# One copy of q, k and v from PSUM to SBUF in layer 1's main loop

## The chip, the cores and the metric

The kernel runs on one core of a Trainium2 chip, as one launch. The metric is the device time of one execution in microseconds. Three executions of the kernel before took 9888.43, 9790.23 and 9846.99 us; their median is 9846.99. A further execution was taken with the hardware profiler, and all durations below come from that one.

## The reference, cut to what matters

The input `x` is four images of 64 x 64 positions with 128 channels, float32. Four layers follow each other:

- Layer 0 is a deformable attention: q, k and v from a 3 x 3 depthwise convolution, offsets from q, gathers of k and v at nine sampled places for each of four heads, a softmax over the nine, and a projection.
- Layer 1 is a linear attention. Of `qkv = x @ w_qkv` it takes a softmax of q over each head's 32 channels, a softmax of k over all 4096 positions, the context `k^T v`, and `context @ q` projected, normalized and added to its input:

```python
q = softmax(q, axis=-1) / sqrt(32)      # 4 heads of 32
k = softmax(k, axis=1)                  # over the positions
context = einsum('bnhd,bnhe->bhde', k, v / n)
out = einsum('bhde,bnhd->bnhe', context, q)
```

- Layer 2 is a gated attention and a mixture of 64 experts with eight positions for each.
- Layer 3 is a causal linear attention and a spectral filter bank (the long convolution with 16 filters).

Every layer works on a normalized input and adds to its residual. The change lies in layer 1.

## The kernel before, in words

**Two streams of work.** `hybrid` runs layer 0 image by image: 8 chunks of 512 positions, four tiles a chunk, four heads a tile, so 128 attention steps an image and 512 in all. I call such a step a group. A group (`attend`, L606 to L662) issues nine gathers on POOL (L619, into one of three `gt` buffers), multiplies and reduces on DVE (L628, L633 to L638), takes one exponential on ACT (`ex`, L642), and multiplies and reduces on DVE again (L646, L651, L654). `front` prepares the next image beside it; it makes two chunks of q (`image`, L462) ahead of the table of k and v (`table`, L422), and the other six behind it.

**The background.** While image b is in layer 0, `Post.run(b - 1)` takes the image before through layers 1 to 3. It is a chain of Python generators; each `yield` hands out a number, the cost of the piece just written, and `hybrid` draws from it until the sum reaches 1176 x (groups so far) / 128, thus 9.19 units a group. Layer 1's loop yields 5.0 in each of its sixteen passes; a chunk of layer 3's attention (L1207 to L1287, eight of them, each with two L1222) yields 5.0 + 4.0 + 4.0. Image 3 has no next image: after its layer 0 the last `Post.run` stands alone (I call it the tail), with `wide` set, which gives it more buffers.

**What sets the order.** The program is written in this interleaved order, but a planner decides at build time in which order each engine's queue holds its instructions: of those whose inputs it takes to be ready it issues first what stands earlier in the text, and an engine that would be idle takes what stands later. On the chip each queue is run in that order. A background that is written early and becomes ready late is therefore issued behind attention groups that stand behind it in the text. At two places the order is tied by hand through `Turns` (L60 to L78): each `ex` is issued on ACT behind the last ACT instruction recorded for "behind" (L640), and the filter bank's copies (L1440) behind that for "samples" (L1439). "Behind" is recorded only while `paced` is set, and that happens at L828, where `stu_tokens` begins, until the image's background ends.

**Layer 1's main loop** (L879 to L915) handles two tiles of 128 positions a pass. PE makes q, k and v of a tile in one matmul into PSUM (`pq`, L883, a bank for each tile; `ps_qkv` has one buffer beside layer 0 and two in the tail). DVE subtracts the maximum from k (L888), ACT takes its exponential (L889). DVE sets a column of ones in `v1` (L891), ACT copies v into it (L892), and PE adds `ek^T v1` to the context (`pc`, L899), so that the column of ones gives the sum of the softmax. For q, DVE reduces the maximum of each head (L895) and subtracts it (L897), ACT takes the exponential (L903), DVE sums, inverts and multiplies (L905 to L907), PE transposes (L910) and ACT copies the result to `qT` (L914). L888, L892, L895 and L897 read `pq` in PSUM.

Of the kernel before, what the change touches and what calls it, by code (L numbers as in the profile page):

```python
# [16 lines left out]
P = 128  # L17
# [3 lines left out]
C = 128  # L21
# [698 lines left out]
class Post:  # L720
# [115 lines left out]
    def layer1(self, xa, xaT, st, xb):  # L836
        nc, k, w = self.nc, self.k, self.w
        with ExitStack() as outer:
            keep = self.pool(outer, "l1keep", 1)
            sm = self.pool(outer, "l1sm", 1)  # L840
            qT = keep.tile([P, N], F32, name="qT")
            w2 = keep.tile([P, C], F32, name="w2")
            with ExitStack() as ctx:
                big = self.pool(ctx, "l1big", 1)
                wk = self.pool(ctx, "l1wk", 2)
                ps = self.psum(ctx, "l1tr", 2, 3)
                ps_qkv = self.psum(ctx, "l1qkv", 1, 2)
                ps_ctx = self.psum(ctx, "l1ctx", 1, 1)
                xT = big.tile([P, N], F32, name="xT1")
                for c in range(8):  # L850
                    part = slice(c * 512, (c + 1) * 512)
                    nc.sync.dma_start(xT[:, part], xaT[:, part])
                yield 5.0
                rs = groupnorm(nc, k, sm, ps, st)
                for h in range(4):
                    part = xT[:, h * 1024 : (h + 1) * 1024]
                    nc.scalar.activation(part, part, AF.Identity, bias=rs[:, 1:2], scale=rs[:, 0:1])
                yield 5.0


                mx = sm.tile([P, 9], F32, tag="mx", name="mx")
                for c in range(8):
                    pk = ps.tile([P, 512], F32, tag="p", name="pk")
                    nc.tensor.matmul(
                        pk, lhsT=w.qkv1[:, C : 2 * C], rhs=xT[:, c * 512 : (c + 1) * 512],
                        start=True, stop=True,
                    )
                    nc.vector.tensor_reduce(mx[:, c : c + 1], pk, AX.X, ALU.max)
                    yield 1.5
                nc.vector.tensor_reduce(mx[:, 8:9], mx[:, 0:8], AX.X, ALU.max)  # L870
                dg = sm.tile([P, P], F32, tag="dg", name="dg")
                nc.vector.tensor_scalar_mul(dg, k.ident, mx[:, 8:9])
                pm = ps.tile([P, 512], F32, tag="p", name="pm")
                nc.tensor.matmul(pm[:, :P], lhsT=k.ones, rhs=dg, start=True, stop=True)
                mrow = sm.tile([P, 1, P], F32, tag="mrow", name="mrow")
                nc.scalar.copy(mrow[:, 0, :], pm[:, :P])


                pc = ps_ctx.tile([P, 512], F32, tag="p", name="pc")  # L879
                for i in range(0, NT, 2):  # L880
                    pq = ps_qkv.tile([P, 2, 512], F32, tag="p", name="pq")
                    for u in range(2):
                        nc.tensor.matmul(  # L883
                            pq[:, u, : 3 * C], lhsT=xT[:, (i + u) * P : (i + u + 1) * P],
                            rhs=w.qkv1, start=True, stop=True,
                        )
                    ek = wk.tile([P, 2, C], F32, tag="ek", name="ek")
                    nc.vector.tensor_sub(ek, pq[:, :, C : 2 * C], mrow.to_broadcast([P, 2, P]))  # L888
                    nc.scalar.activation(ek, ek, AF.Exp)  # L889
                    v1 = wk.tile([P, 2, C + 1], F32, tag="v1", name="v1")  # L890
                    nc.vector.memset(v1[:, :, C : C + 1], 1.0)  # L891
                    nc.scalar.copy(v1[:, :, :C], pq[:, :, 2 * C : 3 * C])  # L892
                    qh = pq[:, :, :C].rearrange("p u (h c) -> p u h c", h=4)
                    qm = wk.tile([P, 2, 4], F32, tag="qm", name="qm")
                    nc.vector.tensor_reduce(qm, qh, AX.X, ALU.max)  # L895
                    eq = wk.tile([P, 2, 4, 32], F32, tag="eq", name="eq")
                    nc.vector.tensor_sub(eq, qh, qm.unsqueeze(3).to_broadcast([P, 2, 4, 32]))  # L897
                    for u in range(2):
                        nc.tensor.matmul(  # L899
                            pc[:, : C + 1], lhsT=ek[:, u, :], rhs=v1[:, u, :],  # L900
                            start=(i + u == 0), stop=(i + u == NT - 1),
                        )
                    nc.scalar.activation(eq, eq, AF.Exp)  # L903
                    qs = wk.tile([P, 2, 4], F32, tag="qs", name="qs")
                    nc.vector.tensor_reduce(qs, eq, AX.X, ALU.add)  # L905
                    nc.vector.reciprocal(qs, qs)
                    nc.vector.tensor_mul(eq, eq, qs.unsqueeze(3).to_broadcast([P, 2, 4, 32]))  # L907
                    pt = ps.tile([P, 512], F32, tag="p", name="pt")
                    for u in range(2):
                        nc.tensor.transpose(  # L910
                            pt[:, u * P : (u + 1) * P], eq[:, u].rearrange("p h c -> p (h c)"),
                            k.ident,
                        )
                    nc.scalar.copy(qT[:, i * P : (i + 2) * P], pt[:, : 2 * P])  # L914
                    yield 5.0  # L915


                rk = sm.tile([P, 1], F32, tag="rk", name="rk")
                nc.vector.reciprocal(rk, pc[:, C : C + 1])
                cx = sm.tile([P, P], F32, tag="cx", name="cx")  # L920
                nc.vector.scalar_tensor_tensor(cx, pc[:, :C], rk, k.heads, ALU.mult, ALU.mult)
                pt = ps.tile([P, 512], F32, tag="p", name="pt")
                nc.tensor.transpose(pt[:, :P], cx, k.ident)
                cxT = sm.tile([P, P], F32, tag="cxT", name="cxT")
                nc.scalar.copy(cxT, pt[:, :P])
                pw = ps.tile([P, 512], F32, tag="p", name="pw")
                nc.tensor.matmul(pw[:, :C], lhsT=cxT, rhs=w.out1, start=True, stop=True)
                nc.scalar.copy(w2, pw[:, :C])
                yield 6.0


            with ExitStack() as ctx:
                yp = self.pool(ctx, "l1y", 2 if self.wide else 1)
                wk = self.pool(ctx, "l1wk2", 2)
                ps = self.psum(ctx, "l1o", 3, 4)
                n2 = self.norm[0]
                for half in range(2):
                    y = yp.tile([P, 16, C], F32, tag="y", name="y")
                    ny = Norm(nc, k, sm, 16, "ny")
                    for c in range(4):  # L940
                        i = 16 * half + 4 * c
                        po = ps.tile([P, 512], F32, tag="p", name="po")
                        for u in range(4):
                            nc.tensor.matmul(
                                po[:, u * P : (u + 1) * P],
                                lhsT=qT[:, (i + u) * P : (i + u + 1) * P], rhs=w2,
                                start=True, stop=True,
                            )
                        nc.vector.tensor_add(
                            y[:, 4 * c : 4 * c + 4, :], po.rearrange("p (u c) -> p u c", u=4),  # L950
                            w.bout.unsqueeze(1).to_broadcast([P, 4, C]),
                        )
                        for u in range(4):
                            ny.add(4 * c + u, y[:, 4 * c + u, :])
                        yield 3.0
                    ny.finish()
                    for c in range(4):
                        x = self.load(wk, xa, 4 * half + c)
                        yc = y[:, 4 * c : 4 * c + 4, :]
                        for u in range(4):  # L960
                            ny.apply(4 * c + u, yc[:, u, :], yc[:, u, :])
                        nc.vector.tensor_mul(yc, yc, w.lns.unsqueeze(1).to_broadcast([P, 4, C]))
                        nc.vector.tensor_add(x, x, yc)
                        for u in range(4):
                            n2.add(16 * half + 4 * c + u, x[:, u, :])
                        nc.sync.dma_start(chunk(xb, 4 * half + c), tiles(x))
                        yield 3.0
                n2.finish()
# [896 lines left out]
```

## Time and profile before

| what | value |
|---|---|
| median of three executions | 9846.99 us |
| profiled execution, its own time | 9880.9 us |
| its span, first to last instruction | 9879.2 us |
| busy PE / weight loads / DVE / ACT / POOL | 5958.9 / 4119.0 / 4642.4 / 2260.0 / 4397.7 us |
| mean granted TensorE clock | 0.761 of full speed |
| first `ex` of images 0, 1, 2, 3 | 272, 1944, 4194, 6461 us |
| layer 1's loop, first to last L883: images 0, 1, 2, 3 of the background | 2010 to 2137, 4292 to 4426, 6560 to 6698, 8674 to 8711 us |

How to read what follows. A line of the groups names source line, engine, operation, output and inputs, their sizes, and the number of instructions, then busy time and mean nanoseconds of one, then how long the engine was idle just before them and what ended that. A line of the timeline gives start and duration in microseconds and, in brackets, the idle time before and its releaser. A line of a source line's own view gives the least, median and greatest duration in nanoseconds. In the table of stages each engine's busy microseconds stand with the number of its instructions, then the granted clock, the share of the DMA engines and their rate.

### The profile page before, as it was taken

The page shows a single profiled execution, that of the slowest core. Times are in us where ns is not written, and L with a number is a line of the kernel's source. Part 1 is how long each engine was busy: PE and PEld are TensorE (multiplying, and loading weights), DVE is VectorE, ACT ScalarE, POOL GpSimd, SP SyncE. Part 2 cuts the span into 40 slices and gives each one's busy share as a digit, 9 for nine tenths or more (in the row PEclk, how much of TensorE's full clock was granted, in tenths as well). Part 3 has the DMA queues.
Part 4 walks back from the last instruction along what each step waited for, and adds up shares of the span by engine and source line. Part 5 has one row for each costly group of instructions (what it writes and reads, how often), then busy time and mean ns, then how long its engine had stood idle before and what let it go on. Part 6 is the DMA issues. An engine that isn't in the chain of part 4 may idle for free.

```text
span 9879.2 us, 87205 instructions
## 1 busy us (share of the span) xinstructions
PE 5958.9 (60%) x30347; PEld 4119.0 (42%) x30347; DVE 4642.4 (47%) x7777; ACT 2260.0 (23%) x4190; POOL 4397.7 (45%) x4736
## 2 busy tenths in 40 slices
PE   7355200056685767756676667744455767757899
PEld 5133100024354545524344445522243555534676
DVE  1545555465454444466454444466454444443222
ACT  3100000023222222223122222213222222232222
POOL 0666666654535455554434445555535445400000
PEclk9677555567787888867787888865677888867999
DMA  6534433334645444454645444444635444444323
GB/s 214 147 111 115 115 103 103 101 105 145 202 123 156 114 115 117 113 140 144 185 140 144 109 114 116 118 135 142 192 117 150 114 111 116 111 136 130 107 68 81
DMA packets 1131344, 1263.41 MB, mean 128 GB/s; under 512 B 392990, under 2 KB 915481, under 8 KB 1126681
## 3 DMA queue, kind: packets, MB, share of 16 engines
q1 hardware_dynamic: 907309, 652.59, 24.1%
q0 software_dynamic: 221184, 604.27, 21.2%
q8 instruction: 240, 3.93, 0.2%
q14 instruction: 199, 1.63, 0.1%
q10 hardware_dynamic: 2412, 0.98, 0.0%
HBM read 1061.76 MB, written 195.61 MB: 127 GB/s over the span
## 4 chain that ended last, share of the span: by engine, by line
PE 34%; another core or an unknown queue 22%; issue 11%; DVE 9%; ACT 7%; POOL 5%; DMA 3%; SPq 1%; DVEq 0%; ACTq 0%; POOLq 0%
PE pa L1450 13%; PE pq L1426 5%; POOL gt L619 5%; ACT y L1440 3%; PE pm L435 2%; DVE o L654 2%; PE ph L1135 1%; DVE pr L628 1%; DMA xin<-x 1%; PE pm L470 1%; DVE s L633 1%; PE pq L883 1%; DVE pv L651 1%; PE pm L512 1%
## 5 line engine op out<-in xcount | busy, mean ns | idle before, releaser
L619 POOL DMA_INDIRECT gt<-tbl,idx x4608 | 4388.7, 952 | 4162.4 <-DVE pv L651 2386.1
L1450 PE MATMUL pa<-y,m 128*128 128x256 f32 x8192 | 2125.9, 412 | 165.8 <-issue 151.4
L1450 PEld LDWEIGHTS pa<-y,m 128*128 128x128 f32 x8192 | 1631.6, 205 | 646.8 <-issue 404.9
L1440 ACT COPY y<-pq 128x1024 f32<-128x1024 f32 x896 | 869.7, 1015 | 2310.4 <-remote 1328.2
L1426 PE MATMUL pq<-th,xh 32*128 32x256 f32 x8192 | 713.1, 452 | 696.8 <-ACT y L1440 473.3
L646 DVE TENSOR_TENSOR qa<-cw,ex 128x36 f32<-128x36 f32 x512 | 104.0, 203 | 2160.0 <-ACT ex L642 1967.3
L654 DVE TENSOR_REDUCE o<-pv 128x32 f32<-128x1152 f32 x512 | 1076.2, 2102 | 12.8 <-remote 9.7
L435 PE MATMUL pm<-wd,xT 128*128 128x256 f32 x2376 | 661.1, 424 | 279.1 <-ACT kv L446 178.0
L1426 PEld LDWEIGHTS pq<-th,xh 32*128 32x128 f32 x8192 | 430.8, 209 | 909.5 <-ACT y L1440 516.6
L628 DVE TENSOR_TENSOR pr<-gt,qa 128x1152 f32<-128x1152 f32 x512 | 690.4, 1348 | 219.2 <-DMA gt<-tbl,idx 186.3
L651 DVE TENSOR_TENSOR pv<-gt,qa 128x1152 f32<-128x1152 f32 x512 | 691.8, 1351 | 35.7 <-DVE qa L646 14.7
L633 DVE TENSOR_REDUCE s<-pr 128x36 f32<-128x1152 f32 x512 | 687.8, 1343 | 0.6
L435 PEld LDWEIGHTS pm<-wd,xT 128*128 128x128 f32 x2376 | 484.0, 212 | 459.8 <-ACT kv L446 202.6
L642 ACT ACTIVATE ex<-sc,mx 128x9 f32<-128x9 f32 x512 | 156.8, 306 | 1125.3 <-DVE mx L638 508.8
L1437 DVE COPY y<-pq 128x1024 f32<-128x1024 f32 x128 | 156.8, 1225 | 466.0 <-ACT y L1440 466.0
L470 PE MATMUL pm<-xT,wd 128*128 128x512 f32 x576 | 294.2, 661 | 133.4 <-issue 76.5
L588 PE MATMUL qa<-sident,qt 128*128 128x128 f32 x256 | 54.4, 340 | 456.8 <-issue 324.5
L1135 PE MATMUL ph<-w,pooled 128*1 128x512 f32 x512 | 238.3, 781 | 46.9 <-DMA w<-in_L_ffn_weight_dram 35.1
L588 PEld LDWEIGHTS qa<-sident,qt 128*128 128x128 f32 x256 | 45.2, 235 | 476.7 <-issue 336.5
L1149 DVE TENSOR_TENSOR g<-pt,b1T 128x16 f32<-128x16 f32 x64 | 11.2, 175 | 487.7 <-PE pt L1144 406.4
L670 PE MATMUL pt<-ident,o 128*128 128x128 f32 x128 | 31.6, 336 | 335.5 <-DVE o L661 118.0
L147 ACT ACTIVATE ln<-xin,ln,ln 128x128 f32<-128x128 f32 x512 | 211.3, 483 | 98.9 <-DMA xin<-x 67.7
(377 smaller groups left out, 6514.4 us busy)
## 6 DMA issues: line engine op xcount, KB each, us to landing
w<-in_L_ffn_weight_dram SPq DMA_DIRECT2D x512, 256.0 KB
th<-th SPq DMA_DIRECT2D x512, 256.0 KB
gt<-tbl,idx POOLq DMA_INDIRECT x4608
xin<-x SPq DMA_DIRECT2D x224, 256.0 KB
x<-xin SPq DMA_DIRECT2D x160, 256.0 KB
tbl<-kv SPq DMA_DIRECT2D x264, 128.0 KB
th<-wx SPq DMA_DIRECT2D x32, 1024.0 KB
q<-qd SPq DMA_DIRECT2D x288, 64.0 KB
```

Source lines behind the costliest of these rows:

```text
L147: self.nc.scalar.activation(dst, src, AF.Identity, bias=self.shift[:, i : i + 1], scale=self.rstd[:, i : i + 1])
L435: nc.tensor.matmul(pm[:, t, :], lhsT=self.xf[:, at : at + P], rhs=self.wd[:, tap, C:], start=(t == 0 and tap == 0), stop=False,)
L470: nc.tensor.matmul(pv, lhsT=self.wd[:, tap, :C], rhs=self.xT[:, 8 * c + dy : 8 * c + dy + 8, dx : dx + HW], start=(tap == 0), stop=False,)
L619: nc.gpsimd.indirect_dma_start(out=gt[:, i, :], out_offset=None, in_=self.tbl[b % 2][:, :], in_offset=bass.IndirectOffsetOnAxis(ap=blk.idx ...
L628: nc.vector.tensor_mul(pr, corners[:, :, 0:32], qa[:, q0 + 32 * g : q0 + 32 * g + 32].unsqueeze(1).to_broadcast([P, 4 * K2, 32]),)
L633: nc.vector.tensor_reduce(s4, pr, AX.X, ALU.add)
L651: nc.vector.tensor_mul(pv, corners[:, :, 32:64], aw.unsqueeze(2).to_broadcast([P, 4 * K2, 32]),)
L654: nc.vector.tensor_reduce(o[:, t, 32 * g : 32 * g + 32], pv.rearrange("p i s -> p s i"), AX.X, ALU.add)
L1135: nc.tensor.matmul(ph[32 * j : 32 * j + 1, :], lhsT=pooled[:, 16 * j + q : 16 * j + q + 1], rhs=w1s[j], start=True, stop=True,)
L1426: nc.tensor.matmul(pq[:, r // 2, r % 2, :, pair, :], lhsT=xh[rows, 2 * (q % 4) + pair, :], rhs=t[rows, 2 * (q % 2) + pair, :].rearrange("p ...
L1440: nc.scalar.copy(to, src)
L1450: nc.tensor.matmul(pa[:, h * 2 * P : (h + 1) * 2 * P].rearrange("p (g x) -> p g x", g=8), lhsT=s.m[u][:, KC * kc + i, :], rhs=yv[:, i], st ...
```

## The change

Two buffers `qkv0` and `qkv1` of 2 x 385 elements in each partition are made before the loop, and their last column is set to one there. In each pass ACT copies q, k and v of both tiles (2 x 384 elements) from PSUM into one of them in turn. The steps that read `pq` now read that buffer, v with its column of ones is a part of it, and the tile `v1` with its memset and its copy is gone. All source lines behind the loop stand four lines further down.

```diff
+                qkv = [big.tile([P, 2, 3 * C + 1], F32, name=f"qkv{i}") for i in range(2)]
+                for t in qkv:
+                    nc.vector.memset(t[:, :, 3 * C :], 1.0)
                 pc = ps_ctx.tile([P, 512], F32, tag="p", name="pc")
                 for i in range(0, NT, 2):
                     pq = ps_qkv.tile([P, 2, 512], F32, tag="p", name="pq")
...
+
+                    sb = qkv[i // 2 % 2]
+                    nc.scalar.copy(sb[:, :, : 3 * C], pq[:, :, : 3 * C])
                     ek = wk.tile([P, 2, C], F32, tag="ek", name="ek")
-                    nc.vector.tensor_sub(ek, pq[:, :, C : 2 * C], mrow.to_broadcast([P, 2, P]))
+                    nc.vector.tensor_sub(ek, sb[:, :, C : 2 * C], mrow.to_broadcast([P, 2, P]))
                     nc.scalar.activation(ek, ek, AF.Exp)
-                    v1 = wk.tile([P, 2, C + 1], F32, tag="v1", name="v1")
-                    nc.vector.memset(v1[:, :, C : C + 1], 1.0)
-                    nc.scalar.copy(v1[:, :, :C], pq[:, :, 2 * C : 3 * C])
-                    qh = pq[:, :, :C].rearrange("p u (h c) -> p u h c", h=4)
+                    v1 = sb[:, :, 2 * C :]
+                    qh = sb[:, :, :C].rearrange("p u (h c) -> p u h c", h=4)
                     qm = wk.tile([P, 2, 4], F32, tag="qm", name="qm")
```

## The prediction

> **What bounds the kernel now.** I read the page first, then the busy time of each engine by stage, then the times of one instruction that every attention step issues (`ex`, L642, 512 of them), then the loop that the change edits. I call one `ex` a group and count them from 0; image b of layer 0 owns groups 128b to 128b+127. From the page:
>
> ```profile
> PE 34%; another core or an unknown queue 22%; issue 11%; DVE 9%; ACT 7%; POOL 5%; DMA 3%; SPq 1%; DVEq 0%; ACTq 0%; POOLq 0%
> L619 POOL DMA_INDIRECT gt<-tbl,idx x4608 | 4388.7, 952 | 4162.4 <-DVE pv L651 2386.1
> L1440 ACT COPY y<-pq 128x1024 f32<-128x1024 f32 x896 | 869.7, 1015 | 2310.4 <-remote 1328.2
> ```
>
> No engine owns the chain. POOL, which issues layer 0's gathers, is idle as long as it works, and most of that idle time ends when the attention's DVE step L651 hands a buffer back. The stages, with each engine's busy time and the granted clock:
>
> ```profile
> core 0: us, PE busy (x) PEld busy (x) DVE busy (x) ACT busy (x) POOL busy (x), PEclk, DMA share, GB/s
> 272.00:1943.00 1671.00, 431.67 (x1295) 273.52 (x1295) 912.77 (x1291) 107.19 (x371) 1095.27 (x1151) 0.61 0.39 112
> 1944.00:4194.00 2250.00, 1498.20 (x7528) 1025.24 (x7528) 1103.93 (x1860) 585.81 (x1075) 1108.39 (x1166) 0.78 0.48 132
> 4292.00:4460.00 168.00, 94.80 (x319) 55.21 (x318) 108.88 (x255) 42.09 (x112) 86.73 (x91) 0.73 0.31 90
> 5103.00:5220.00 117.00, 105.97 (x570) 75.72 (x568) 76.74 (x222) 47.91 (x94) 8.72 (x9) 0.97 0.22 66
> 8674.00:8718.00 44.00, 37.21 (x166) 22.76 (x164) 33.97 (x116) 23.70 (x67) 0.00 (x0) 1.00 0.76 228
> ```
>
> Row 1 is image 0, with no layers 1 to 3 behind it: 1671 / 127 = 13.2 us a group, POOL busy 66%. Row 2 is image 1 with the background: 17.6 us a group, no engine above 67%. So the background is paid as delay in queues, not as work on a full engine. Row 3 is the edited loop of the second background image, row 5 the same loop in the tail, where layer 0 is over. Row 4 is the important one: POOL does 8.7 us of work in 117. The chain there, in order of time:
>
> ```profile
> 5102.69 0.30 ACT L642 ACTIVATE ex<-sc,mx 128x9 f32<-128x9 f32 x1
> ...
> 5220.32 0.30 ACT L642 ACTIVATE ex<-sc,mx 128x9 f32<-128x9 f32 x1
> ...
> 5223.44 0.94 POOL L619 DMA_INDIRECT gt<-tbl,idx  x1 [106.83 <-DVE pv L651]
> ```
>
> This is the hold. From `stu_tokens` on (L828 sets `paced`) each `ex` stands on ACT's queue behind the background's last ACT instruction, so at group 310 the attention stands still until all of layer 3 is through: 117.6 us for one group, with 16 L1222, two to a chunk, so eight chunks of layer 3. The other images have the same hold: 2870.29 to 2971.35 (101.1 us, six chunks) and 7293.82 to 7421.51 (127.7 us, seven). What lies in a hold is background that came late.
>
> **The edited loop, priced.**
>
> ```profile
> L883 PE MATMUL pq<-wqkv,xT x256: 486/840/1006, 2011.0 to 8711.7; 128*128 128x384 f32 x128
> L892 ACT COPY v<-pq x64: 352/356/378, 2024.5 to 8713.0; 128x256 f32<-128x256 f32 x64
> L897 DVE TENSOR_TENSOR eq<-pq,qm x64: 364/417/426, 2025.4 to 8714.6; 128x256 f32<-128x256 f32 x64
> L907 DVE TENSOR_TENSOR eq<-eq,qs x64: 394/419/478, 2032.3 to 8716.3; 128x256 f32<-128x256 f32 x64
> ...
> 8709.72 0.41 DVE L897 TENSOR_TENSOR eq<-pq,qm 128x256 f32<-128x256 f32 x1
> 8710.05 0.19 DVE L906 RECIPROCAL qs<-qs 128x8 f32<-128x8 f32 x1
> 8710.27 0.43 DVE L907 TENSOR_TENSOR eq<-eq,qs 128x256 f32<-128x256 f32 x1
> 8710.61 0.42 DVE L905 TENSOR_REDUCE qs<-eq 128x8 f32<-128x256 f32 x1
> ```
>
> *Copy.* 64 copies of 256 elements (356 ns) become 64 of 768. The 1024-element copy at L1440 takes 1015 ns, so 356 + 512 x (1015 - 356) / 768 = 795 ns: 64 x 0.44 = 28 us more on ACT. ACT is busy 26% of image 1's stretch and 54% in the tail's loop, so I charge nothing for the work itself; without that cover it costs 28 us. But every DVE step of the loop now queues behind this copy, and the copy behind whatever ACT has ahead of it, a waiting `ex` included; that delay is in the loop terms below.
>
> *DVE's sources.* Three of its steps a pass read SBUF in place of PSUM. L897 (PSUM) lets the next start after 0.33 us, L907 (SBUF) after 0.34; durations 417 and 419. I charge 0. [...]
>
> *Memsets.* 64 of 60 ns become 8; they lie in DVE's idle time, 0 (at most 4 us).
>
> *PSUM comes free early.* `pq` has one buffer while layer 0 runs. Before, the next L883 waits for L897 (in row 3's stretch PE waited 10.6 us for it in five waits); after, for the copy alone, and two `qkv` buffers let a second pass start. This matters through the planner. With the two programs laid side by side, engine by engine, the changed one issues the loop differently: for image 1 still two passes a group, for images 2 and 3 sixteen passes within groups 264 to 268 and 392 to 396 (nine and seven in the densest), where they filled 265 to 273 and 393 to 402. What follows moves forward, and at the hold two of eight chunks of layer 3 already stand ahead of it for image 2, four of eight for image 3 (one before); image 1's hold keeps its six. From group 311 and 439 on, the ACT order of the background is the old one.
>
> **The sum.**
>
> 1. *Holds.* Five chunks leave them (two, three). In the hold a chunk takes (117.6 - 13.2) / 8 = 13.1 us, so 65 us go. Beside attention they cost something: the first 52 groups of the second background image take 17.2 us each, 4.0 over the quiet 13.2, and carry 9.19 units of the program's own pacing (1176 / 128); a chunk has 13 units (5 + 4 + 4), so 5.7 us each, 28 back. Net -37. The other end: the 101.1 us hold has two chunks less than the 117.6 one and is only 16.5 shorter, 8.3 a chunk, net -13. I take -37, since it is the mean of the very stretch that shrinks.
> 2. *Dense loops.* What sixteen passes cost above quiet groups: image 1, 147.8 us for ten groups, 16 over; image 2, 167.3 for nine, 48 over; image 3, 171.4 for ten, 39 over. A dense loop has no row beside attention; the nearest is the tail, where a pair of passes takes 4.84 us (L888 at 8701.27 and 8706.11), 16 x 2.42 = 39. Image 2: 39 - 48 = -9; image 3: 0. The low end is image 1's 16 (-32 and -23, together -55), the high end below (+28 and +37, together +65).
> 3. *Image 1's loop.* Same spacing: 0. Its 16 us could vanish (-16), or the copy's 0.8 us could show in each pass (+13).
> 4. *Tail loop.* DVE idles about 0.8 us in each 4.84 us pair, waiting for ACT and PE; steady order one pass at a time, -2 (0 to -5).
> 5. *Table loads.* The exp, square root and gelu steps change places once more each way on ACT for image 2: 2 x 1.28 = +3.
>
> Together -37 - 9 + 0 - 2 + 3 = -45. Against the profiled execution's own 9880.9 us that is 9836. It lay 34 above the median of the three runs (9847.0), so the forecast is **9802 us**. The runs spread over 98 us, so a change under about 1% can hardly be told from none.
>
> **Rivals.**
>
> *A: dense matmuls make the loop cheap.* For: L883 takes 840 ns at the median and 486 in the tail, and the granted clock is 0.73 in row 3, 1.00 in row 5. If the dense loop runs as in the tail and hides beside attention as image 1's does, the low end of term 2 holds: 9802 - 46 = 9756. Against: DVE needs 16 x 2.29 us (five steps of 0.42 and one of 0.19) beside four attention steps of 6.9 (L651, L628, L633 and L654: 1.35 + 1.35 + 1.34 + 2.10, and 0.8 of small ones). Chance 0.20. [...]
>
> *B (slower): the dense loop holds the attention.* DVE runs in order, and in group 265 some thirty loop steps now stand between the attention's L628 and L638. At the cold pace PE needs 2.90 + 1.23 + 0.63 = 4.76 us a pass (the rows at 4311.71, 4309.77 and 4310.79), 76 us for sixteen, all of it added if POOL's three buffers are full meanwhile: +65 for the two images, +13 for image 1, holds at their low end -13, so +65: 9912. It decides from a pass of about 3.8 us on (61 us for sixteen, then term 2 is +35 and outweighs the holds). Chance 0.20.
>
> *C: nothing moves.* The work that leaves a hold reappears in full before it, as 17.6 us a group whatever the spacing: 9847. Chance 0.12.
>
> [...] Chance 0.03.
>
> Forecast: 0.45. The range takes A and most of B, with the spread of the runs: 9705 to 9930. Faster by over 1% (under 9749) needs A and a lucky median: 0.20. Slower by over 1% (over 9945) needs B with more than its price, or a stall that the rows don't show: 0.12. Within 1%: 0.68.
>
> **What the profile after would show.** the new copy near 795 ns x64; the steps of L895 and L897 still 417 ns; the hold of image 2 near 90 us, image 3's near 90, image 1's still 101; sixteen passes of images 2 and 3 in some 60 us and the clock above 0.73 there; the tail's pair at 4.5 to 4.8 us. I am wrong if a group in 264 to 268 lasts over 45 us (B), or if the holds shrink and the groups ahead of them grow by as much (C).

## The result: 0.5% faster, and the profile after

| | before | after |
|---|---|---|
| median, same chip | 9869.34 us | 9813.69 us |
| lowest and highest of 19 executions each | 9790.23, 9919.02 | 9775.16, 9850.76 |
| span of the profiled execution | 9879.2 us | 9819.3 us |

The ratio is **0.9947, with a 95% interval of 0.9926 to 0.9968**: 56 us less. That is under the 1% that I took for the bound of what can be told, but with this many executions the interval stays clear of 1. Forecast were 45 us less.

The changed kernel's page, its span, its chain and its two costliest groups (columns as explained above; lines behind the loop are four higher):

```profile
span 9819.3 us, 87113 instructions
...
PE 33%; another core or an unknown queue 26%; issue 12%; DVE 9%; ACT 7%; POOL 6%; DMA 4%; SPq 1%; DVEq 0%; ACTq 0%; POOLq 0%
...
L619 POOL DMA_INDIRECT gt<-tbl,idx x4608 | 4389.1, 953 | 4114.9 <-DVE pv L651 2351.1
...
L1444 ACT COPY y<-pq 128x1024 f32<-128x1024 f32 x896 | 869.5, 1015 | 2279.5 <-remote 1318.7
```

The shape is that of before: POOL idles nearly as long as it works, and most of its idle time still ends at L651. POOL's idle time is 47.5 us shorter (4162.4 before), most of what the span lost. The table of stages of the changed kernel: image 0 alone, image 1 with the background, the groups 264 to 267 that hold the loop of the second background image, the holds of images 2 and 3, and the loop in the tail:

```profile
core 0: us, PE busy (x) PEld busy (x) DVE busy (x) ACT busy (x) POOL busy (x), PEclk, DMA share, GB/s
272.00:1941.00 1669.00, 425.86 (x1295) 271.36 (x1295) 913.53 (x1292) 107.28 (x371) 1097.13 (x1152) 0.61 0.39 112
1942.00:4193.00 2251.00, 1487.16 (x7531) 1021.22 (x7532) 1101.07 (x1847) 592.10 (x1077) 1106.38 (x1162) 0.79 0.47 131
4299.00:4398.00 99.00, 67.77 (x255) 40.42 (x254) 67.89 (x163) 40.53 (x91) 43.15 (x45) 0.83 0.22 68
5111.00:5212.00 101.00, 90.48 (x455) 62.00 (x454) 64.05 (x188) 40.29 (x81) 8.97 (x9) 0.96 0.21 66
7316.00:7386.00 70.00, 47.38 (x275) 37.59 (x274) 41.86 (x117) 26.51 (x52) 8.70 (x9) 0.91 0.19 59
8624.00:8663.00 39.00, 35.79 (x166) 22.28 (x164) 33.75 (x103) 30.18 (x67) 0.00 (x0) 0.98 0.88 264
```

The same four groups (264 to 267) in the kernel before, where eight copies of v (L892) start in them instead of sixteen of `qkv`:

```profile
4292.00:4364.00 72.00, 39.67 (x112) 21.69 (x111) 48.13 (x104) 20.72 (x53) 41.91 (x45) 0.69 0.29 86
```

PE's work in these groups went from 39.7 us to 67.8, the granted clock from 0.69 to 0.83, and the stretch from 72 us to 99. Rows four and five are the holds. In order of time, in the changed kernel, the `ex` of images 2 and 3 ahead of the hold and behind it, and POOL's first gather afterwards with its idle time:

```profile
5110.69 0.30 ACT L642 ACTIVATE ex<-sc,mx 128x9 f32<-128x9 f32 x1 [2.89 <-DVE mx L638]
...
5211.78 0.30 ACT L642 ACTIVATE ex<-sc,mx 128x9 f32<-128x9 f32 x1
...
5214.89 0.94 POOL L619 DMA_INDIRECT gt<-tbl,idx  x1 [90.35 <-DVE pv L651]
...
7315.65 0.30 ACT L642 ACTIVATE ex<-sc,mx 128x9 f32<-128x9 f32 x1 [3.24 <-DVE mx L638]
...
7385.91 0.30 ACT L642 ACTIVATE ex<-sc,mx 128x9 f32<-128x9 f32 x1
...
7388.20 0.94 POOL L619 DMA_INDIRECT gt<-tbl,idx  x1 [59.12 <-DVE pv L651]
```

Image 2's hold is 101.1 us long (117.6 before), image 3's 70.3 (127.7 before, where POOL idled 115.51 us). The whole account, from the starts of `ex` in both profiles; the last column has the same differences on another chip, between the kernel whose order up to the tail is that of before (e_tail below) and the changed kernel (after_again):

| stretch (groups) | before | after | difference | on another chip |
|---|---|---|---|---|
| image 1: loop (128 to 140) | 215.0 | 221.7 | +6.7 | -13.5 |
| image 1: ahead of the hold (140 to 181) | 711.6 | 707.4 | -4.2 | -8.0 |
| image 1's hold (181) | 101.1 | 101.5 | +0.4 | -0.2 |
| image 2: loop (256 to 273) | 265.4 | 278.3 | +12.9 | +17.7 |
| image 2: ahead of the hold (273 to 309) | 643.1 | 639.9 | -3.2 | -17.5 |
| image 2's hold (309) | 117.6 | 101.1 | -16.5 | -16.5 |
| image 3: loop (384 to 402) | 267.9 | 278.4 | +10.6 | +23.4 |
| image 3: ahead of the hold (402 to 437) | 564.7 | 591.6 | +26.9 | -0.5 |
| image 3's hold (437) | 127.7 | 70.3 | -57.4 | -45.9 |
| the rest of layer 0, where the order is the same | 5332.7 | 5309.2 | -23.5 | +1.9 |
| tail | 1260.1 | 1246.9 | -13.2 | -5.0 |
| sum | | | -60.5 | -64.1 |

In both pairs the holds shrink by as much as the total or more (-73.5 and -62.6) and the dense loops take some of it (+23.5 and +41.1). The 23.5 us of the unchanged stretches in the first pair lie within what executions of one kernel differ by (129 us between the lowest and the highest before), so of that pair's 60 us some 24 are placed by the order (all rows but these and the tail's); in the second pair nearly all are. Ahead of image 3's hold the first pair lost 26.9 us and the second nothing. In that stretch the first pair has groups of over 28 us, three before (408, 416, 432) and six after (404, 416, 420, 422, 425, 432); the second has none.

### The profile page after: what moved, and what is told of

Same layout as the page of the kernel before. It is cut to its first block, busy times and chain, and to the rows that moved or that the text cites. A ratio compares the mean times of both kernels' runs of the same rounds, so it can differ in the third digit from the quotient of the medians.

```text
span 9819.3 us, 87113 instructions
## 1 busy us (share of the span) xinstructions
PE 5912.5 (60%) x30347; PEld 4102.3 (42%) x30347; DVE 4635.2 (47%) x7721; ACT 2288.4 (23%) x4192; POOL 4398.1 (45%) x4736
## 4 chain that ended last, share of the span: by engine, by line
PE 33%; another core or an unknown queue 26%; issue 12%; DVE 9%; ACT 7%; POOL 6%; DMA 4%; SPq 1%; DVEq 0%; ACTq 0%; POOLq 0%
PE pa L1454 13%; POOL gt L619 6%; PE pq L1430 5%; ACT y L1444 4%; PE pm L435 2%; DVE o L654 2%; PE ph L1139 1%; DVE pr L628 1%; DMA gt<-tbl,idx 1%; DVE s L633 1%; DVE pv L651 1%; PE pm L470 1%; DMA xin<-x 1%; PE pa L1250 1%
## 5 line engine op out<-in xcount | busy, mean ns | idle before, releaser
L1444 ACT COPY y<-pq 128x1024 f32<-128x1024 f32 x896 | 869.5, 1015 | 2279.5 <-remote 1318.7
L654 DVE TENSOR_REDUCE o<-pv 128x32 f32<-128x1152 f32 x512 | 1076.2, 2102 | 8.5 <-DVE qa L646 2.7
L435 PE MATMUL pm<-wd,xT 128*128 128x256 f32 x2376 | 653.8, 422 | 278.4 <-ACT kv L446 193.9
L628 DVE TENSOR_TENSOR pr<-gt,qa 128x1152 f32<-128x1152 f32 x512 | 690.1, 1348 | 253.2 <-DMA gt<-tbl,idx 232.5
L651 DVE TENSOR_TENSOR pv<-gt,qa 128x1152 f32<-128x1152 f32 x512 | 691.8, 1351 | 24.0 <-DVE qa L646 8.6
L147 ACT ACTIVATE ln<-xin,ln,ln 128x128 f32<-128x128 f32 x512 | 211.2, 482 | 97.8 <-DMA xin<-x 77.0
```

The costliest lines, as they stand in the source:

```text
L147: self.nc.scalar.activation(dst, src, AF.Identity, bias=self.shift[:, i : i + 1], scale=self.rstd[:, i : i + 1])
L435: nc.tensor.matmul(pm[:, t, :], lhsT=self.xf[:, at : at + P], rhs=self.wd[:, tap, C:], start=(t == 0 and tap == 0), stop=False,)
L628: nc.vector.tensor_mul(pr, corners[:, :, 0:32], qa[:, q0 + 32 * g : q0 + 32 * g + 32].unsqueeze(1).to_broadcast([P, 4 * K2, 32]),)
L651: nc.vector.tensor_mul(pv, corners[:, :, 32:64], aw.unsqueeze(2).to_broadcast([P, 4 * K2, 32]),)
L654: nc.vector.tensor_reduce(o[:, t, 32 * g : 32 * g + 32], pv.rearrange("p i s -> p s i"), AX.X, ALU.add)
L1444: nc.scalar.copy(to, src)
```

## The experiments

The main comparison and the last group of four experiments were run on chips where the kernel before takes about 9870 us; the others ran on two chips where the kernel before takes 7799.05 and 7795.84 us, so each ratio is taken against the kernel before on the same chip, and only differences are carried across.

My theory, H: the gain is the shorter holds, and they are shorter because `pq` comes free early, so that the planner issues the loop sooner. The rivals, as letters in the expectations: P, the packed passes themselves pay; M, the memsets; T, the tail; D, DVE's steps gain by reading SBUF in place of PSUM; N, the holds cost nothing; E, the copy pays because ACT does it; and L, which was formed on the way, that what counts is how late the background is at the point where the attention is first tied to it.

| run | edit in a word | ratio (95%) | us | hold of image 2, 3 |
|---|---|---|---|---|
| e_psumsrc | k and q read from PSUM again | 0.9979 (0.9969 to 0.9989) | -18 | 114.6, 113.5 |
| e_onebuf | one `qkv` buffer | 0.9948 (0.9931 to 0.9964) | -40 | 95.8, 70.6 |
| e_narrow | not in the tail | 0.9923 (0.9906 to 0.9939) | -56 | 95.5, 70.7 |
| e_ones | only the column of ones is set once | 1.0013 (1.0002 to 1.0023) | +9 | 114.6, 123.4 |
| after_again | the changed kernel | 0.9910 (0.9893 to 0.9926) | -69 | 97.5, 70.7 |
| e_tail | only in the tail | 0.9995 (0.9985 to 1.0005) | -2 | 114.0, 116.6 |
| b_nohold | before, `paced` set later | 1.0009 (0.9999 to 1.0018) | +6 | 93.9, 102.0 |
| a_nohold | after, `paced` set later | 0.9941 (0.9921 to 0.9961) | -46 | 86.3, 59.4 |
| b_late28w | before, the tie two groups later | 0.9931 (0.9909 to 0.9953) | -71 | 103.8, 94.6 |
| a_late28w | after, the tie two groups later | 0.9843 (0.9822 to 0.9864) | -164 | 92.1, 25.3 |
| a_late46w | after, the tie three groups later | 0.9859 (0.9837 to 0.9881) | -142 | 104.7, 32.9 |
| e_dvecopy | the copy on DVE | 0.9966 (0.9947 to 0.9984) | -35 | 101.1, 74.1 |

Microseconds are differences of medians within a group; the groups are the first four, the next four, the last four.

### Which part of the change pays

**e_psumsrc.** The copy stays, but DVE reads k and q from `pq` as before, so that `pq` is held as long as ever.

```diff
-                    nc.vector.tensor_sub(ek, sb[:, :, C : 2 * C], mrow.to_broadcast([P, 2, P]))
+                    nc.vector.tensor_sub(ek, pq[:, :, C : 2 * C], mrow.to_broadcast([P, 2, P]))
...
-                    qh = sb[:, :, :C].rearrange("p u (h c) -> p u h c", h=4)
+                    qh = pq[:, :, :C].rearrange("p u (h c) -> p u h c", h=4)
```

> The copy of q, k and v and the column of ones stay as in the change, but DVE's steps for q and k read PSUM again, so that PSUM is freed as late as before. The planned order falls back to that of before: two passes a group in images 2 and 3, eight chunks of layer 3 in the hold of image 2 and seven in that of image 3. Theory H (the gain is layer 3 leaving the holds because PSUM comes free early): holds near 118 and 128 us again, nothing gained, 0 to +20 us against the kernel before (28 us more ACT work, beside other work). Rival O (one wide copy in place of a copy and a memset is what pays): half or more of the 56 us stays. The DVE steps take 417 ns from either memory, so rival D (SBUF sources) would show as a longer median of these steps here than in the change.

The planned order falls back to two passes a group, the holds to six, eight and seven chunks, and most of the gain goes; 18 us stay (interval -24 to -9), which H did not give it. By one profile of each, e_psumsrc is 8.5 us shorter than e_tail in image 1's loop (groups 128 to 140) and 6.2 us between it and the hold; the cause was not settled. In its trace, POOL's first gather behind the holds of images 2 and 3:

```profile
4091.27 0.94 POOL L619 DMA_INDIRECT gt<-tbl,idx  x1 [103.76 <-DVE pv L651]
...
5696.44 0.94 POOL L619 DMA_INDIRECT gt<-tbl,idx  x1 [96.11 <-DVE pv L651]
```

The changed kernel on a chip of the same speed (after_again) has these lines instead:

```profile
4066.75 0.94 POOL L619 DMA_INDIRECT gt<-tbl,idx  x1 [87.21 <-DVE pv L651]
...
5656.68 0.94 POOL L619 DMA_INDIRECT gt<-tbl,idx  x1 [59.74 <-DVE pv L651]
```

So the bank's early release changes the order, and with the order go the holds. Whether the order alone would do it, with the bank held as long as before, was not tested.

**e_onebuf.**

```diff
-                qkv = [big.tile([P, 2, 3 * C + 1], F32, name=f"qkv{i}") for i in range(2)]
+                qkv = [big.tile([P, 2, 3 * C + 1], F32, name=f"qkv{i}") for i in range(1)]
...
-                    sb = qkv[i // 2 % 2]
+                    sb = qkv[0]
```

> The change with one qkv buffer instead of two. The planned loop is less dense (3 to 5 passes a group in images 2 and 3 instead of up to 9 and 7), but the holds have the same six and four chunks as in the change. Theory H: holds near 101 and 70 us as in the change, and the loop stretches of images 2 and 3 cost less than the change's 278 and 278 us (5 to 15 us each), so -55 to -75 us against before. Rival P (the second buffer and the dense loop are what pays): half or more of the gain goes, -30 us or less.

Two to five passes a group now, and the holds are as short as with two buffers. But the loops did not get cheaper by being spread: groups 256 to 273 took 232.7 us and 384 to 402 247.9 (235.3 and 244.8 in after_again), and PE's idle time ahead of L886 that ended with the copy went from 42.3 us to 107.9. The gain, -40 us beside the -56 of e_narrow on the same chip, is less than H gave and more than P: the early release carries most of it, and the second buffer perhaps the rest (the two intervals overlap a little).

**e_narrow and e_tail.** The old and the new form of the loop stand under a condition:

```diff
+                    if not self.wide:
+                        sb = qkv[i // 2 % 2]
+                        nc.scalar.copy(sb[:, :, : 3 * C], pq[:, :, : 3 * C])
...
+                    else:
+                        ek = wk.tile([P, 2, C], F32, tag="ek", name="ek")
+                        nc.vector.tensor_sub(ek, pq[:, :, C : 2 * C], mrow.to_broadcast([P, 2, P]))
```

> The change in the three loops beside layer 0 only; the tail keeps the old loop. The planned order up to the tail is that of the change. Theory H: the holds as in the change (101, 70 us), the start of the tail as early as in the change (45 us or so before that of the kernel before), and only the tail's 13 us missing: -35 to -50 us. Rival T (the tail loop, which lies alone on the path, brings most): less than half of the gain, -25 us or less.

> The change in the tail only; the three loops beside layer 0 keep the old loop, and the planned order up to the tail is that of before: holds with six, eight and seven chunks. Theory H: holds near 96, 115 and 114 us as before, only the tail's share, 0 to -13 us. Rival T (the tail loop, alone on the path, brings most): -28 us or more.

(e_tail has the condition the other way round.) Without the tail's part the gain is -56 us, with the tail's part alone -2: the tail pays next to nothing, and T falls. (The -56 lies a little beyond the 35 to 50 that I expected.)

**e_ones.** The kernel before with two `v` buffers whose last column is set once:

```diff
+                vs = [big.tile([P, 2, C + 1], F32, name=f"vs{i}") for i in range(2)]
+                for t in vs:
+                    nc.vector.memset(t[:, :, C:], 1.0)
...
-                    v1 = wk.tile([P, 2, C + 1], F32, tag="v1", name="v1")
-                    nc.vector.memset(v1[:, :, C : C + 1], 1.0)
+                    v1 = vs[i // 2 % 2]
```

> The kernel before with only the column of ones moved: two v buffers with the column set once, v copied as before, q and k from PSUM. The planned order is that of before but for one chunk: the hold of image 3 has eight chunks of layer 3 instead of seven, that of image 2 eight as before. Theory H: holds near 118 and 135 to 140 us, 0 to +15 us against before. Rival M (the 56 memsets that go out of the loop pay): -5 us or more, with the holds as before.

The memsets are worth nothing, and M falls; the 9 us on the other side go with one more chunk of layer 3 in image 3's hold, 123.4 us against the 116.6 of e_tail, whose order up to the tail is that of before (135 to 140 were expected).

**e_dvecopy.**

```diff
-                    nc.scalar.copy(sb[:, :, : 3 * C], pq[:, :, : 3 * C])
+                    nc.vector.tensor_copy(sb[:, :, : 3 * C], pq[:, :, : 3 * C])
```

> The change with its copy on DVE instead of ACT. The planned loop is the densest of all (14 passes in one group), the holds have six, six and four chunks as in the change. 64 copies of 768 elements on DVE, at the 0.33 us that 256 take from one start to the next about 0.8 us each, 53 us of DVE work in all. Theory L: holds near 95, 97 and 70 us as in the change, so most of the gain stays; the loops cost 10 to 20 us more each and the tail 10: -15 to -45 us against before. Rival E (ACT's nearness or idleness is what pays): nothing left, 0 us or slower.

The DVE copy takes 959 ns, 64 of them 61 us on the engine that the attention needs, and the kernel is still 35 us faster than before, with the holds that the table shows. Group 264 takes 53.2 us and group 392 53.6 here. E falls: which engine frees the bank matters little for the holds.

**after_again**, the changed kernel beside these on another chip:

> The changed kernel itself, beside the others of this call. Its planned order up to the tail is that of the kernel that keeps the old loop in the tail, which took 0.9923 of the kernel before. Theory H: holds of 95 to 101 us with six chunks (images 1 and 2) and 70 us with four (image 3), -50 to -65 us against before. Rival T (the tail brings more): -75 us or more.

Here 69 us go (interval -83 to -58; expected were 50 to 65), where the main comparison has 56, from a total that is a fifth shorter. A gain in per cent would have scaled with the total; this one did not. That fits with a hold having hardly any gathers in it (POOL worked 9 of 101 us).

### Is it the holds, or what stands behind them?

**b_nohold and a_nohold** set `paced` later, so that `ex` is tied to the background only from the filter bank on:

```diff
-            self.paced = True
             yield from self.stu_tokens(stu, xa, self.u[b % 2], xb)
+        self.paced = True
         yield from self.stu_filters(stu, self.u[b % 2], xb, out[b])
```

> The kernel before with the tie of each ex to the background set one stage later, where the filter bank begins and no longer where the token stage begins: in the planned order layer 3's chunks lie one or two to a group in 310 to 316 (182 to 188, 437 to 444), and the eight token steps come at once at group 316 instead. Theory H: no group above 60 us at 181, 309 and 437; a chunk beside attention costs some 5 us where it took 9.5 to 14 in the hold, and a new, shorter hold of about 45 us for the token steps comes at 316: -20 to -100 us against before. Rival N (a hold costs nothing, since the attention makes up for it afterwards): within 15 us of before.

> The changed kernel with the same later tie. Theory H: with no hold for layer 3 to leave, the change is worth less than half of what it is with the hold: -5 to -25 us against the kernel before with the later tie (whose run is in the same call). Rival P (the gain comes from the loop itself, wherever layer 3 ends): -45 us or more against it.

This is the experiment that went against H as I had worded it. If the tie at L828 made the hold, the kernel before should gain by losing it, and the change should have little left to bring. Neither came: the change still brings 52 us, which is the number that rival P gave for this run. But P's reason fails, for the loops cost more here as well (+16.9 us in groups 264 to 273 and +24.3 in 392 to 402). The holds at 181, 309 and 437 do vanish in the kernel before (14.9 to 17.1 us remain), and new ones stand where the tie now begins, at groups 187, 315 and 443, of 85.5, 93.9 and 102.0 us. The time is within 6 us of before, which is what N gave; but N's reason is wrong, for the idle time is there, in another place. POOL's gathers behind the new holds of images 2 and 3 in b_nohold:

```profile
4176.24 0.94 POOL L619 DMA_INDIRECT gt<-tbl,idx  x1 [82.05 <-DVE pv L651]
...
5784.04 0.94 POOL L619 DMA_INDIRECT gt<-tbl,idx  x1 [90.50 <-DVE pv L651]
```

In a_nohold, with the change:

```profile
4155.49 0.94 POOL L619 DMA_INDIRECT gt<-tbl,idx  x1 [72.49 <-DVE pv L651]
...
5741.98 0.94 POOL L619 DMA_INDIRECT gt<-tbl,idx  x1 [48.30 <-DVE pv L651]
```

The change again takes the most from image 3's (102.0 to 59.4 us), and 50 us from the three together. Hence theory L: a hold is the background's lateness, paid at the first place where the attention is tied to it, wherever that is; the change makes the background less late.

**b_late28w, a_late28w, a_late46w** test L without touching the loop. An idle piece of 28 (or 46) units ahead of layer 3, with as much added to the total, lets two (or three) more groups stand ahead of the tie in the text, while a background that is late catches up:

```diff
             yield from self.layer2_ffn(xa, xb)
+            yield 28.0
             yield from self.layer3_attn(xb, xa)
...
-WORK = 1176.0
+WORK = 1204.0
```

> The kernel before, its loop untouched, with a pause of 28 units (three groups of attention) written between layer 2 and layer 3, and the pacing stretched by the same 28 units. In the planned order the hold of image 1 keeps six chunks, that of image 2 has six instead of eight and that of image 3 five instead of seven. Theory L (what pays is how late the background is where the attention is first tied to it, whatever shortens that): holds near 95, 97 and 85 us, -25 to -50 us against before, without any change of the loop. Rival P (the gain comes from the loop itself): within 15 us of before, since the same work is only moved.

> The changed kernel with the same pause of 28 units. Planned holds: six, six and two chunks. Theory L: holds near 95, 97 and 40 us; only image 3's gains, -15 to -35 us against the changed kernel (0.987 to 0.989 of the kernel before, where the change has 0.991). Rival G (the filter bank, which gets three groups less, gives it all back): 0.991 or more.

> The changed kernel with a pause of 46 units, five groups. Planned holds: five, five and one chunk. Theory L: holds near 85, 85 and 25 us, -30 to -65 us against the changed kernel (0.983 to 0.987 of the kernel before) unless the filter bank, with five groups less, gives part back; rival G: 0.991 or more.

In the kernel before, this edit alone brings -71 us (interval -90 to -46), as much as the whole change and more than I expected, and the holds go from 101.1, 117.6 and 127.7 us to 92.0, 103.8 and 94.6: 56 of it. That bears L out, though the longer total also quickens the pace of the background (9.41 units a group instead of 9.19), which was not tested by itself. On top of the change it gives **0.9843, the fastest median here**, below the changed kernel's 0.9947 with intervals that do not touch. That is about 100 us less, where I had expected 15 to 35. In a_late28w, image 3's hold and the gather behind it:

```profile
7212.28 0.31 ACT L642 ACTIVATE ex<-sc,mx 128x9 f32<-128x9 f32 x1 [2.75 <-DVE mx L638]
...
7237.54 0.29 ACT L642 ACTIVATE ex<-sc,mx 128x9 f32<-128x9 f32 x1
...
7241.59 0.95 POOL L619 DMA_INDIRECT gt<-tbl,idx  x1 [16.05 <-DVE pv L651]
```

It is 25.3 us long, against 70.3 in the changed kernel. The holds of the three images are 64 us shorter in all; the loops' stretches fell too, from 278.3 and 278.4 us to 261.2 and 265.2, in line with before: another 30 us. This profile is of the fastest of five executions (9650.93 us, their median 9706.33). More is not shown to be better: the intervals of 28 and 46 units overlap. The time with 46 units lies where it was expected, but the holds do not: with 46 units the holds of images 1 and 2 lengthened to 103.7 and 104.7 us, though the planned order has one chunk less in them, and the stretch behind them grew (groups 320 to 384: 1042.7 us with 28 units, 1078.0 with 46). Against the holds with 28 units ACT idles longer in them (68.4 and 69.2 us instead of 54.5); the waits that grew most are those of `front`'s copy at L487 (4.1 us to 10.6 and 10.7) and of L147 for the DMA of `xin` (2.8 to 8.6 and 7.8). Why they fall into the hold was not settled.

## Why the prediction was right, and where its terms were off

The forecast of -45 us against -56 measured is right as a sum, of larger terms that were off: the holds by 13 us towards faster, the dense loops by 32 us towards slower (by the rows of the account). In the one pair of profiles they make -27 together, and the stretches that the change does not touch make up the difference; on the other chip what is given back ahead of the holds is less, and the order carries the whole gain (-80 and +41 us, where -37 and -9 were forecast). The direction and the holds as its place were reasoned out; that the sum came so close is in good part luck, in the one pair because stretches that no term names shrank, in the other because two errors of opposite sign cancel.

**Term 1, the holds: right in kind, too small.** Forecast -65 in the holds and 28 given back ahead of them; measured in this pair -73.9 (-16.5 and -57.4) and +23.7 (-3.2 and +26.9). The net is -50 instead of -37. The even price of 13.1 us a chunk was the weak step: two chunks fewer took 16.5 us from image 2's hold (8.3 each, the low end that I named from image 1's row), three fewer took 57.4 from image 3's (19 each). Both holds were to be near 90 us; they are 101.1 and 70.3. Counting chunks is a poor measure of a hold; a_late46w, with fewer chunks and a longer hold, says the same. The 5.7 us for a chunk beside attention is near what the faster chip shows: in after_again the six groups ahead of the holds of images 2 and 3 that carry a chunk take 16.3 us on average and a quiet one 11.4, so 5 each. That the 23.7 us given back here are the chunks' is not shown: they go with the long groups named under the account, and on the other chip these stretches got 18 us shorter.

**Term 2, the dense loops: the step that failed.** Forecast -9 for image 2 and 0 for image 3; measured +12.9 and +10.6 in the account's rows, and +4.4 and +6.9 in the very groups that the forecast counted (264 to 273, 392 to 402). I had charged sixteen passes 39 us over quiet groups, at the tail's pace. The passes themselves came close to the 60 us that the profile was to show: 66.1 and 66.0 us from the first L886 to the last, where L883 took 134.1 and 137.2 before. But the four groups that hold them took 99 and 90 us, and over quiet groups of 13.2 us the loop costs 53 and 46 us instead of 39. On the other chip it costs 40 and 41 over quiet groups of 11.4, as forecast, but there the spread loop costs only 24 and 19 (e_tail), so that the dense one loses 16.5 and 22.0. The clock did rise (0.69 to 0.83, and 0.64 to 0.83 in image 3), as rival A wanted. Even so, the clock was not what decided the loop's cost. DVE's queue in group 264 of the changed kernel, the attention's steps and the loop step that stood in their way (start, duration, engine, line, and in brackets the idle time before):

```profile
4311.07 1.30 DVE L651 TENSOR_TENSOR pv<-gt,qa 128x1152 f32<-128x1152 f32 x1
...
4324.55 0.43 DVE L894 TENSOR_TENSOR ek<-qkv,mrow 128x256 f32<-128x256 f32 x1 [9.82 <-ACT qkv L892]
...
4328.44 1.35 DVE L628 TENSOR_TENSOR pr<-gt,qa 128x1152 f32<-128x1152 f32 x1
...
4335.39 1.30 DVE L633 TENSOR_REDUCE s<-pr 128x36 f32<-128x1152 f32 x1
...
4344.01 0.15 DVE L638 TENSOR_REDUCE mx<-sc 128x1 f32<-128x9 f32 x1
```

First L894 waits 9.82 us for the new copy, with the attention's L654 and L628 behind it on the queue (the input of L654 was written by 4312.4 us, L654 starts at 4325.56). The copy itself had been held up on ACT by something that the profile calls remote:

```profile
4323.72 0.80 ACT L892 COPY qkv<-pq 128x768 f32<-128x768 f32 x1 [9.50 <-remote]
```

Then from L628 to the L638 that its `ex` needs pass 15.6 us, with the loop's steps between them. In the same group of the kernel before it is 7.7 us (4303.81 to 4311.48), and in image 1's group around 2206 us of the changed kernel 4.1 (L628 at 2206.09, L638 at 2210.17). POOL, out of buffers, idles:

```profile
4348.09 0.95 POOL L619 DMA_INDIRECT gt<-tbl,idx  x1 [23.26 <-DVE pv L651]
```

That is rival B's mechanism, and the mark that I set for it, a group over 45 us, was just passed: group 264 took 46.0. On the faster chip (after_again) that group takes 33.7 us, against 21.6 in e_tail: DVE has no wait of over 2 us in it, but from L628 to L638 it is still 13.0 us instead of 7.7. So that wait for the copy shows on the slower chip alone, and the cost of the loop's steps between the attention's on both. B's price, worked out from rows that ran at a granted clock of 0.55 (4305 to 4316 us of the kernel before), did not come, because the other side of the sum was larger: +23.5 for both loops, against 50 from the holds (on the other chip +41 against 80). The loops would have had to cost about twice as much to turn the sign.

**Term 3, image 1's loop:** 0 forecast, between -16 and +13; +6.7 for the loop in this pair, -13.5 on the other chip. Within the bounds, with a sign that differs between the pairs: in the first, two groups (135 and 139) take 60.1 us instead of 34.7.

**Term 4, the tail's loop:** -2 forecast, bounds 0 to -5; in this pair the loop is 5.5 us shorter, just beyond them. Its passes, by the copies in the tail of the changed kernel, follow each other in 2.0 us instead of 2.42:

```profile
8645.01 0.80 ACT L892 COPY qkv<-pq 128x768 f32<-128x768 f32 x1
...
8647.13 0.80 ACT L892 COPY qkv<-pq 128x768 f32<-128x768 f32 x1
...
8649.09 0.80 ACT L892 COPY qkv<-pq 128x768 f32<-128x768 f32 x1
```

The end of the program did not move by as much in e_tail (-2 us, interval -12 to +4), so whether the rest of the 13 us in the account is the change's was not settled.

**Term 5, table loads:** two more of 1.28 us, as forecast.

**Copy, sources and rival D.** The source lines' own views in the changed kernel (least, median and greatest duration in ns):

```profile
L892 ACT COPY qkv<-pq x64: 779/801/809, 2012.2 to 8657.2; 128x768 f32<-128x768 f32 x64
...
L894 DVE TENSOR_TENSOR ek<-qkv,mrow x64: 376/420/427, 2020.7 to 8658.1; 128x256 f32<-128x256 f32 x64
...
L901 DVE TENSOR_TENSOR eq<-qkv,qm x64: 360/419/428, 2018.8 to 8659.3; 128x256 f32<-128x256 f32 x64
```

The copy takes 801 ns (795 forecast). L901 reads SBUF now and takes 419 ns; it took 417 from PSUM. In e_psumsrc, the one-sided case, L894 takes 425 and L901 420 ns from PSUM. With SBUF as the source it is 420 and 419, so these rows differ by 1 to 5 ns. No run shows the gain from SBUF sources that D supposed, and D is out.

**Rival C**, that all of it reappears ahead of the hold: here 23.7 of 73.9 us did at most, on the other chip nothing (-17.5 and -0.5).

**The cause, after all runs.** Freeing `pq` early lets the planner issue the loop sooner, so the background is less late where the attention is tied to it. The first half is shown by e_psumsrc, the second by b_late28w, which makes as large a gain without the loop. What stays open is the 18 us of e_psumsrc, and what sets the length of a hold beside the chunks in it. What I had put down to one tie at L828 belongs to any first tie (b_nohold).

## What to carry to other kernels

Where two streams share queues and are tied at some points, look for the place where one stream stands still on every engine; the other stream is late there, and a change far upstream that frees a single-buffered PSUM bank a little earlier can shorten it (here from 117.6 to 101.1 us and from 127.7 to 70.3). Taking the tie away only moved the wait to the next tie here (b_nohold: 85.5, 93.9 and 102.0 us there); placing it where more of the other stream is done shortened it (56 us off the three holds and 71 off the total here, for two lines). Price such a wait by when its work comes ready, and not by the number of instructions in it.

## What the runs showed that was not expected

**The same program takes 21% less on another chip** (7799.05 against 9869.34 us), nearly all of it where gathers run. Image 0, with no background, takes 13.2 us a group on one and 11.4 on the other, and the groups behind the last hold (438 to 511) 1198 and 823 us, while the tail (1260.1 and 1252.2) and the holds (101.1, 117.6 and 127.7, and 95.5, 114.0 and 116.6 in e_tail) are much closer. On the slower chips the chain has 22% (before), 26% (after) and 21% (a_late28w) at "another core or an unknown queue"; after_again's page has none of it, and POOL's idle time is 2027 us instead of 4115:

```profile
POOL 31%; PE 26%; issue 15%; DVE 10%; DMA 10%; ACT 4%; SPq 0%; DVEq 0%; POOLq 0%; ACTq 0%
...
L619 POOL DMA_INDIRECT gt<-tbl,idx x4608 | 4392.4, 953 | 2026.6 <-issue 1336.5
...
L1444 ACT COPY y<-pq 128x1024 f32<-128x1024 f32 x896 | 868.7, 1013 | 1073.0 <-PE pq L1430 1070.0
```

A gather takes 953 ns on both and the filter bank's copy 1015 and 1013; what differs is what ends most of the wait ahead of the copy: "remote" on the one (1318.7 us), PE on the other (1070.0 us). What the unknown queue is, the traces do not say, and whether it is the chip or something that ran beside the kernel was not tested. The gain of the change was about the same in microseconds on both (-56 and -69), as the holds shrink alike on both (-16.5 and -57.4, and -16.5 and -45.9).

**A source in PSUM cost DVE nothing** at 256 float32 elements a partition: 417 ns from PSUM and 419 from SBUF for the same subtraction (L897 before, L901 after).
